# Masks of two query blocks made piece by piece between the steps of a graph attention layer

## The chip, the cores and the metric

The kernel runs on 1 core of a Trainium2 chip. The metric is device time in microseconds (us) of one execution, the median of several runs. Engines are TensorE (PE, matrix products and transposes), VectorE (DVE), ScalarE (ACT), GpSimd (POOL) and SyncE (SP, which here issues most DMA transfers).

## The reference

Eight graphs of 2048 nodes with 256 channels share one adjacency matrix of 2048 x 2048. For each graph, masked self-attention of 8 heads, then a residual, a layer norm, a feed-forward block of two layers, a second residual and norm, and an outer residual and norm:

```python
qkv = jnp.einsum('fnc,ck->fnk', x, w_qkv)            # f 8, n 2048, c 256
scores = jnp.einsum('fnhd,fmhd->fhnm', q, k) / jnp.sqrt(D)
scores = jnp.where((adj > 0)[None, None], scores, -1e9)
attn = softmax(scores, axis=-1)
t = jnp.einsum('fhnm,fmhd->fnhd', attn, v).reshape(F, N, C)
x1 = layernorm(x + t)
x2 = layernorm(x1 + relu(x1 @ w1 + b1) @ w2 + b2)
out = layernorm(x + x2)
```

The mask is the same for all graphs and heads. The kernel needs it turned: key nodes on the partitions, query nodes along the row.

## The kernel before

**Steps.** The work is cut into 1024 items `(f, qc, g, mb)`: 8 graphs `f`, 4 query blocks `qc` of 512 nodes, 2 groups `g` of 4 heads, 16 key blocks `mb` of 128 nodes. One pass of the main loop is one step `t`; a graph is 128 steps (`FRAME`), a group 16. In step `t` the kernel first lets waiting side work go on (`advance`), then issues the exponentials of item `t+1` (ACT, L237), the score products of item `t+2` (PE, L230; VectorE adds the mask to the scores as it moves them out of PSUM, L233, in two halves), the products with the values of item `t` (PE, L249), and the summing of the exponentials for the denominators (`add_up`): some blocks added by POOL (L271), some by an accumulating DMA that POOL issues (`p<-p`, L268), for `mb` 4, 5, 7, 9, 11 and 13.

**Side work.** Turning the input, projecting queries, keys and values, denominators, division, norms and the feed-forward block are Python generators kept in the list `fill`, sorted by due step. `start(t, gen, due)` adds one. A generator yields a number (go on so many steps later), `BANK` (it wants the spare PSUM bank, of which the main loop leaves one, so at most one such unit starts per step), `MORE` (it holds that bank and has more matmuls) and a few other conditions. `advance` hands out work as long as a credit of TensorE time lasts (`STEP` is added per step). With `finish=True` the credit is not asked. Nothing of this runs on the chip: it sets the order in which each engine's instructions stand, and every engine takes its own in that order. SP's transfers stand in one such order too, and a transfer that must wait holds up those behind it.

**When side work begins.** The table `NEXT` names the steps of a graph in which units for the next graph are started: turns of the input (`turn`), query projections (`ask`), key and value projections of node block `c` and group `g` (`project`). `kp` and `vp` hold 11 key and 11 value tiles in rotation, 8 for a graph and 3 of the next one.

**Masks.** `begin` (L559) makes the masks before the loop. For each of the 16 squares `(qc, c)` of 512 x 512 an SP transfer loads the adjacency into a `p` tile (L565), VectorE turns it into a code in bf16 (L582, two instructions), and `mask_blocks` (L132) transposes it on PE in two banks of eight 128 x 128 blocks (L141), moved out as 8-bit codes by ACT (L147) and VectorE (L145), and stored to the DRAM buffer `MD` (L148). While `qc` is 0 and 1, the turns and projections of the first graph stand between the squares; after `(1, 3)` the scores of the first two items and the first exponential are issued, and then follow the eight squares of `qc` 2 and 3 by themselves. The first query block's masks stay in SBUF; the others are fetched from `MD` by `load_mask` (L150), for query block `qc+1` in every second step of `qc`'s second group (`mb` odd, L607).

**Outcome.** When a block of queries is done, `outcome` (L333) takes a `y` tile (two in the pool), and `tail` (L359) runs its norms and `feed_forward` through the spare bank: two transposes of `y`, two units of the first layer, two of the second.

Of the kernel before, what the change touches and what calls it, by code (L numbers as in the profile page):

```python
# [10 lines left out]
F32 = mybir.dt.float32  # L11
BF16 = mybir.dt.bfloat16
I32 = mybir.dt.int32
I8 = mybir.dt.int8
F8 = mybir.dt.float8e5
AF = mybir.ActivationFunctionType
ALU = mybir.AluOpType
AX = mybir.AxisListType

P = 128  # L20
H = 8
D = 32
CH = 512
# [6 lines left out]
BANK, MORE, WAIT, TURNED, ROOM, INPUTS = -1, -2, -3, -4, -5, -10  # L30
STEP, UNIT, TURN, KEPT = 2200, 1024, 1400, 2200

MASKED = -57344.0
CODE = -5.0
# [27 lines left out]
def fast_path(ctx, tc, cst, x, adj, out, RS):  # L62
    nc = tc.nc
    F, N, C = x.shape
    NCK, TPC, MB = N // CH, CH // P, N // P
# [5 lines left out]
    kp = ctx.enter_context(tc.tile_pool(name="kp", bufs=3 * NCK - 1))  # L71
    qp = ctx.enter_context(tc.tile_pool(name="qp", bufs=4))
    vp = ctx.enter_context(tc.tile_pool(name="vp", bufs=3 * NCK - 1))
    pp = ctx.enter_context(tc.tile_pool(name="pp", bufs=12))
    work = ctx.enter_context(tc.tile_pool(name="work", bufs=1))
    yp = ctx.enter_context(tc.tile_pool(name="yp", bufs=2))
# [25 lines left out]
    def bank(dt=F32):  # L102
        shape = [P, CH] if dt == F32 else [P, 2, CH]
        if state["side"] is not None:
            i = 1 - state["side"]
            return ps_x[i].tile(shape, dt, name=f"x{i}")
        i = state["turn"]
        state["turn"] = (i + 1) % 5
        pool = ps_s[i] if i < 3 else ps_x[i - 3]
        return pool.tile(shape, dt, name=f"s{i}" if i < 3 else f"x{i - 3}")  # L110
# [11 lines left out]


    MD = dp.tile([NCK, MB // 2, P, 2 * CH // 4], I32, name="md")
    MK = {}

    def words(mask):
        return mask.rearrange("p b q -> p (b q)").bitcast(I32)
# [5 lines left out]
    def mask_blocks(qc, mc, cv, to=None):  # L134
        for half in range(2):
            yield BANK
            ps = bank(BF16)
            for r in range(2):
                for j in range(TPC):
                    rr = 2 * half + r  # L140
                    nc.tensor.transpose(ps[:, r, j * P:(j + 1) * P], cv[:, j, rr * P:(rr + 1) * P], identb)  # L141
            k = 2 * mc + half
            m = to[half] if to else mask_piece(0, qc, k)
            if half:
                nc.vector.tensor_tensor(m, ps, cst["ones"][:, 0:1, None].to_broadcast([P, 2, CH]), ALU.min, saturate=False)  # L145
            else:
                nc.scalar.copy(m.bitcast(I8), ps)  # L147
            nc.sync.dma_start(MD[qc, k], words(m))  # L148

    def load_mask(f, qc, k):  # L150
        nc.sync.dma_start(words(mask_piece(f, qc, k)), MD[qc, k])
# [343 lines left out]
    def start(t, gen, due):  # L495
        fill.append([t, gen, 1, due])
        fill.sort(key=lambda e: e[3])
# [13 lines left out]
    def advance(t, finish=False):  # L511
        state["credit"] = min(max(state["credit"], 0) + STEP, KEPT)
        state["now"] = t
        free = not state["holder"]

        def more():
            if state["holder"] and state["holder"][2] == WAIT:
                return False
            due = [e[3] for e in fill if e[2] == BANK and e[0] <= t or e is state["holder"]]
            return finish or state["credit"] >= UNIT or min(due) <= t  # L520

        if state["holder"]:
            resume(state["holder"], t)
            while state["holder"] and more():
                resume(state["holder"], t)
        inputs = True
        for e in list(fill):
            while e[2] is not None and e[0] <= t and e is not state["holder"]:
                if e[2] == BANK:
                    if not free or not more():  # L530
                        break
                    free = False
                elif e[2] < INPUTS:
                    inputs = inputs and not any(u is not None for u in live[:INPUTS - e[2]])
                    if not inputs:
                        break
                elif e[2] == TURNED and state["turned"] or e[2] == ROOM and state["tails"] == 2:
                    break
                resume(e, t)
            while e is state["holder"] and more():  # L540
                resume(e, t)
# [6 lines left out]
    def ask(f, c):  # L548
# [5 lines left out]
            60: [(project, 1, 0)], 66: [(ask, 3)], 72: [(turn, 3)], 80: [(project, 2, 0)], 98: [(ask, 0)], 100: [(project, 3, 0)],  # L554
            104: [(project, 0, 1)], 108: [(project, 1, 1)], 112: [(project, 2, 1)], 116: [(project, 3, 1)]}

    def begin():
        todo = deque((qc, c) for qc in range(NCK) for c in range(NCK))
        rows, cols = [], deque()  # L559

        def fetch():
            if todo:
                qc, c = todo.popleft()
                t = pp.tile([P, 4, CH], F32, name="p").bitcast(I32)
                nc.sync.dma_start(t, adj[qc * CH:(qc + 1) * CH, c * CH:(c + 1) * CH].rearrange("(j p) m -> p j m", p=P))  # L565
                cols.append((qc, c, t))

        for c in range(NCK):
            rows.append(pp.tile([P, 4, CH], F32, name="p"))
            xc = rows[c][:, 0:2, :].rearrange("p a (b c) -> p (a b) c", c=C)  # L570
            nc.sync.dma_start(xc, x[0, c * CH:(c + 1) * CH, :].rearrange("(j p) c -> p j c", p=P))
            fetch()
        fetch()
        while cols:
            qc, c, col = cols.popleft()
            if c % 2 == 0:
                two = pp.tile([P, 4, CH], F32, name="p").rearrange("p a q -> p (a q)").bitcast(BF16)
            cv = two[:, c % 2 * TPC * CH:(c % 2 + 1) * TPC * CH].rearrange("p (j m) -> p j m", m=CH)

            for half, what in enumerate((CODE, MASKED)):  # L580
                part = slice(half * 2 * P, (half + 1) * 2 * P)
                nc.vector.tensor_scalar(cv[:, :, part], col[:, :, part], 0.0, what, op0=ALU.is_le, op1=ALU.mult)  # L582
            fetch()
            xT = rows[c][:, 2:4, :]
            if qc == 0:
                yield from turn_rows(rows[c][:, 0:2, :].rearrange("p a (b c) -> p (a b) c", c=C), xT)
                nc.sync.dma_start(XD[0][c], xT)
                XT[0, c] = xT
                if c == 0:
                    yield from queries(0, 0, xT)  # L590
                yield from project(0, c, 0, xT)
            elif qc == 1:
                yield from project(0, c, 1, xT)
            if qc and c % 2 == 0:
                out4 = take([P, 4, 2, CH], F8)
                give(out4)
            yield from mask_blocks(qc, c, cv, [out4[:, c % 2 * 2 + i] for i in range(2)] if qc else None)
            if (qc, c) == (1, NCK - 1):
                for k in range(LEAD):
                    scores(items[k])  # L600
                exponentials(items[0])

    for _ in begin():
        pass
    state["side"] = 0
    for t, (f, qc, g, mb) in enumerate(items):
        if g == 1 and mb % 2 and (f + 1 < F or qc + 1 < NCK):  # L607
            load_mask(f + (qc + 1) // NCK, (qc + 1) % NCK, mb // 2)
        for what, *which in NEXT.get(t % FRAME, []):
            to = f if what is ask and which[0] else f + 1  # L610
            if to < F:
                at = (0, 0, 0) if what is turn else (which[0], 0, 0) if what is ask else (0, which[1], which[0] * TPC)
                start(t, what(to, *which), t + 3 * MB if what is turn else items.index((to, *at)) - LEAD - 1)
        if t == len(items) - MB // 2:
            xr, xb = state["rows"] = [take([P, TPC, C], F32) for _ in range(2)]
            nc.sync.dma_start(xr, x[f, qc * CH:(qc + 1) * CH, :].rearrange("(p j) c -> p j c", p=P))
        if t == len(items) - 2:
            nc.gpsimd.tensor_tensor(xb, xr, rows(cst["be2r"]), ALU.add)
        if t:
            advance(t)  # L620

        if t + 1 < len(items):
            exponentials(items[t + 1])
        if t + LEAD < len(items):
            nf, _, ng, nmb = items[t + LEAD]
            t0 = t
            while (nf, nmb // TPC, ng) not in V:
                advance(t0, finish=True)
                t0 += 1
            scores(items[t + LEAD])  # L630
        values(items[t])
        add_up(items[t])
        if mb == LAST and t + 1 < len(items):
            start(t + 2, denominator(f, qc, g, t + SUM), t + SUM + 4)
        if t == len(items) - 3:
            start(t, denominator(f, qc, g, t), t)
# [245 lines left out]
```

## Time and profile before

| | us |
|---|---|
| median of 3 runs | 3190.41 (3189.46 to 3194.38) |
| the profiled execution | 3196.28 |
| its span, first to last instruction | 3194.5 |
| TensorE busy (mean granted clock 0.987) | 3081.7 |
| VectorE busy | 2749.6 |
| ScalarE busy | 2417.7 |
| GpSimd busy | 2593.3 |

The profile page shows one execution: the busy share of each engine, the span in 40 slices with a digit for tenths, the DMA queues, the groups of instructions by line with count, busy time, mean length in ns, and the idle time before them with what ended it. The timeline lists instructions by start and length. The chain that ended last covers only the last microseconds here, with 0% at every name, so the stages are read from windows and from the timeline. Times of one step are differences between the starts of successive exponentials (L237).

### The profile page before, as it was taken

Reading aid. Unit: us, or ns where it says so; the run is one execution under the profiler, and the core shown is the slowest. Engines: PE = TensorE matmul, PEld = TensorE weight load, DVE = VectorE, ACT = ScalarE, POOL = GpSimd, SP = SyncE. Lnnn points to the kernel's source line nnn. Section 1 sums busy time; section 2 is a strip of 40 time slices with the busy share of each in tenths; the row PEclk is TensorE's granted clock in tenths of the full one; section 3 lists DMA queues with packets and bytes.
Section 4 is the critical chain, followed back from the end, with each engine's and each line's share of the span. In section 5 each row is a group of like instructions: output and inputs, shape, how many; then the busy total and the mean of one; then the engine's idle time right before and its main releaser. Section 6 shows DMA issues by size and latency. Waiting matters only on the chain. (4 is left out here: it accounts for less than half of the span.)

```text
span 3194.5 us, 68226 instructions
## 1 busy us (share of the span) xinstructions
PE 3081.7 (96%) x28868; PEld 963.0 (30%) x28868; DVE 2749.6 (86%) x3139; ACT 2417.7 (76%) x1909; POOL 2593.3 (81%) x1361
## 2 busy tenths in 40 slices
PE   7899999999999999999999999999999999999985
PEld 4222333222332223332333323323233233332222
DVE  4798988888889988889988988988988888889985
ACT  3677778777787777788777788778778778777774
POOL 0578888788888888888888888888889788889875
PEclk8899999999999999999999999999999999999998
DMA  9688889788798888898888899888879788888872
GB/s 323 142 192 193 183 175 199 161 188 189 179 195 188 191 194 178 176 204 196 187 177 174 194 208 198 168 182 196 196 174 203 177 196 192 176 177 166 178 150 64
DMA packets 153096, 589.46 MB, mean 185 GB/s; under 512 B 15024, under 2 KB 67760, under 8 KB 103888
## 3 DMA queue, kind: packets, MB, share of 16 engines
q0 software_dynamic: 64128, 433.22, 68.8%
q1 hardware_dynamic: 87840, 150.50, 13.7%
q8 instruction: 228, 3.74, 0.4%
q10 hardware_dynamic: 816, 1.31, 0.1%
q14 instruction: 84, 0.69, 0.1%
HBM read 146.67 MB, written 37.75 MB: 58 GB/s over the span
## 5 line engine op out<-in xcount | busy, mean ns | idle before, releaser
L233 DVE TENSOR_TENSOR p<-s,mask 128x1024 f32<-128x1024 f32 x2048 | 2409.1, 1218 | 325.0 <-PE s L230 182.9
L237 ACT ACTIVATE p<-p 128x2048 f32<-128x2048 f32 x1024 | 1956.0, 1910 | 566.5 <-DVE p L233 481.1
L271 POOL TENSOR_TENSOR p<-p 128x2048 f32<-128x2048 f32 x382 | 1875.4, 4909 | 359.1 <-ACT p L237 358.8
L230 PE MATMUL s<-qT,kT 32*128 32x512 f32 x8192 | 1172.5, 642 | 44.2 <-DVE p L233 39.4
L249 PE MATMUL x<-p,v 128*32 128x512 f32 x8192 | 1093.5, 606 | 4.6 <-ACT p L237 4.6
L230 PEld LDWEIGHTS s<-qT,kT 32*128 32x128 f32 x8192 | 320.9, 183 | 671.3 <-DVE p L233 643.6
L268 POOL DMA_DIRECT2D p<-p x382 | 416.8, 1092 | 70.1 <-ACT p L237 46.4
L249 PEld LDWEIGHTS x<-p,v 128*32 128x32 f32 x8192 | 161.5, 108 | 784.0 <-issue 310.2
L315 PE MATMUL x<-p,halves 128*32 128x512 f32 x2080 | 269.9, 595 | 0.0
L54 PE MATMUL x<-in,wqkv 128*32 128x512 f32 x1888 | 245.7, 592 | 0.0
L290 ACT ACTIVATE y<-y,nb,rs 128x256 f32<-128x256 f32 x372 | 219.1, 591 | 6.1 <-POOL nb L287 5.9
L278 DVE BATCH_NORM_STATS2 st<-y 128x6 f32<-128x256 f32 x372 | 155.0, 417 | 1.8 <-POOL y L370 1.8
L54 PE MATMUL x<-turned,w1s 128*32 128x512 f32 x992 | 123.9, 593 | 0.0
L54 PE MATMUL x<-w2s,hT 128*32 128x256 f32 x2016 | 121.8, 382 | 0.0
L54 PEld LDWEIGHTS x<-wqkv,in 128*32 128x32 f32 x3584 | 102.2, 110 | 64.1 <-issue 55.9
L54 PE MATMUL x<-wqkv,in 128*32 128x128 f32 x3584 | 117.4, 273 | 0.0
L315 PEld LDWEIGHTS x<-p,halves 128*32 128x32 f32 x2080 | 67.9, 111 | 156.9 <-issue 155.5
L368 POOL TENSOR_TENSOR y<-y,g2r 128x1024 f32<-128x1024 f32 x31 | 101.6, 3278 | 6.4 <-ACT y L290 6.4
L54 PEld LDWEIGHTS x<-in,wqkv 128*32 128x32 f32 x1888 | 61.3, 110 | 141.3 <-issue 116.5
L284 POOL TENSOR_TENSOR rs<-rs,mhalf 128x4 f32<-128x4 f32 x93 | 96.3, 1035 | 7.8
L370 POOL TENSOR_TENSOR y<-y,be2r 128x1024 f32<-128x1024 f32 x30 | 94.6, 3155 | 0.4
L54 PEld LDWEIGHTS x<-w2s,hT 128*32 128x32 f32 x2016 | 65.9, 111 | 70.7 <-issue 38.5
(121 smaller groups left out, 1301.1 us busy)
## 6 DMA issues: line engine op xcount, KB each, us to landing
p<-p POOLq DMA_DIRECT2D x382, 1024.0 KB, 10.0
in<-xd SPq DMA_DIRECT2D x87, 512.0 KB, 8.9
mask<-md SPq DMA_DIRECT2D x248, 128.0 KB, 8.6
y<-in_x_dram POOLq DMA_DIRECT2D x61, 512.0 KB, 10.1
p<-in_adj_dram SPq DMA_DIRECT2D x16, 1024.0 KB, 9.3
out_dram<-y SPq DMA_DIRECT2D x31, 512.0 KB, 6.2
in<-in_x_dram SPq DMA_DIRECT2D x30, 512.0 KB, 10.6
xd<-in SPq DMA_DIRECT2D x28, 512.0 KB, 8.8
```

Source lines behind the costliest of these rows:

```text
L54: nc.tensor.matmul(out[r:r + D], lhsT[:, r:r + D], rhs, start=start, stop=stop)
L230: nc.tensor.matmul(ps2[half][:, j, :], KT[f, mb // TPC, g][r:r + D, (mb % TPC) * P:(mb % TPC + 1) * P], QT[f, qc, g][r:r + D, :], start=Tr ...
L233: nc.vector.tensor_tensor(pt[:, 2 * half:2 * half + 2, :], ps, MK[f, qc, mb // 2][:, mb % 2, None, :].to_broadcast([P, 2, CH]), ALU.add)
L237: nc.scalar.activation(PT[item], PT[item], AF.Exp, scale=1.0 / math.sqrt(D))
L249: nc.tensor.matmul(O[grp][r:r + D, :], V[f, mb // TPC, g][:, mb % TPC, r:r + D], PT[item][:, h, :], start=(mb == 0), stop=(mb == LAST))
L268: nc.gpsimd.dma_start(PT[f, qc, g, chain[0]], PT.pop(item), accum_op=ALU.add)
L271: nc.gpsimd.tensor_tensor(first, first, PT.pop(item), ALU.add)
L278: nc.vector.bn_stats(st, t[:, j, :])
L284: nc.gpsimd.tensor_tensor(rs, rs, cst["mhalf"], ALU.pow)
L290: nc.scalar.activation(t[:, j, :], t[:, j, :], AF.Identity, bias=nb[:, j:j + 1], scale=rs[:, j:j + 1])
L315: nc.tensor.matmul(ps[r:r + D, :], cst["halves"][:, g, :], term[:, h, :], start=(n == 0), stop=(n == len(blocks) - 1))
L368: nc.gpsimd.tensor_tensor(z, z, rows(cst["g2r"]), ALU.mult)
```

## The change

The squares of query blocks 2 and 3 leave `begin`. They are made instead in 32 pieces of 512 queries x 128 keys by a new generator, `mask_job`, started every 2.25 steps from step 2 of the first graph. A piece works in one of four spare buffers, taken from a `spare` list: one key tile, one value tile, and the two halves of one `y` tile. It loads 128 keys of 512 rows of the adjacency (SP), three steps later casts the integers to bf16 in place (ACT), transposes four blocks through the spare bank (PE), makes the code (VectorE, into a part of the same buffer) and stores it to `MD` (SP); three steps later the buffer goes back. For the second sixteen pieces only the key and the value tile go back, so that the `y` tile is free for the second block's outcome. `MADE` lists the masks that stand in `MD`; before `load_mask` the loop runs `advance` with `finish=True` until the two it needs are in it. In the first graph the table `LATER` takes the place of some entries of `NEXT`: key and value projections begin up to 20 steps later.

```diff
-    MK = {}
+    MK, MADE, spare = {}, {(qc, b) for qc in range(2) for b in range(MB)}, deque()
...
+    def mask_job(n):
+        while not spare:
+            yield 1
+        part = spare.popleft()
+        qc, b = divmod(n + 2 * MB, MB)
+        col = part.bitcast(I32).rearrange("p (j m) -> p j m", j=TPC)
+        nc.sync.dma_start(col, adj[qc * CH:(qc + 1) * CH, b * P:(b + 1) * P].rearrange("(j p) m -> p j m", p=P))
+        yield 3
+        cv = part.bitcast(BF16)[:, 0:CH]
+        nc.scalar.copy(cv, part.bitcast(I32))
+        yield 1
+        yield BANK
+        ps = bank(BF16)[:, 0, :]
+        state["credit"] -= TURN // 2
+        for j in range(TPC):
+            nc.tensor.transpose(ps[:, j * P:(j + 1) * P], cv[:, j * P:(j + 1) * P], identb)
+        m = part[:, CH // 2:3 * CH // 4].bitcast(F8)
+        nc.vector.tensor_scalar(m.bitcast(I8), ps, 0.0, CODE, op0=ALU.is_le, op1=ALU.mult)
+        yield 1
+        nc.sync.dma_start(MD[qc, b // 2, :, b % 2 * P:(b % 2 + 1) * P], m.bitcast(I32))
+        MADE.add((qc, b))
+        yield 3
+        if n < MB or any(part is u for u in parts[0:2]):
+            spare.append(part)
...
+    LATER = {80: [], 100: [(project, 2, 0)], 104: [(project, 3, 0)], 108: [(project, 0, 1)], 112: [(project, 1, 1)],
+             116: [(project, 2, 1)], 120: [(project, 3, 1)]}
+
     def begin():
-        todo = deque((qc, c) for qc in range(NCK) for c in range(NCK))
+        todo = deque((qc, c) for qc in range(2) for c in range(NCK))
...
+    n_mask = 0
+    both = yp.tile([P, TPC, C], F32, name="y").rearrange("p j c -> p (j c)")
+    parts = [kp.tile([P, CH], F32, name="kT"), vp.tile([P, TPC, P], F32, name="v").rearrange("p j c -> p (j c)"),
+             both[:, 0:CH], both[:, CH:2 * CH]]
+    spare.extend(parts)
     for t, (f, qc, g, mb) in enumerate(items):
         if g == 1 and mb % 2 and (f + 1 < F or qc + 1 < NCK):
+            t0 = t
+            while not {((qc + 1) % NCK, b) for b in (mb - 1, mb)} <= MADE:
+                advance(t0, finish=True)
+                t0 += 1
             load_mask(f + (qc + 1) // NCK, (qc + 1) % NCK, mb // 2)
-        for what, *which in NEXT.get(t % FRAME, []):
+        while n_mask < 2 * MB and t >= 2 + 9 * n_mask // 4:
+            start(t, mask_job(n_mask), 3 * MB - 2 + n_mask if n_mask < MB else 4 * MB - 2 + n_mask)
+            n_mask += 1
+        for what, *which in (NEXT if f else {**NEXT, **LATER}).get(t % FRAME, []):
```

## The prediction

> **What bounds the kernel now.** I read the page's slices first, then a table of windows, the timeline of the opening, the groups by line, and last the DMA section. The slices:
>
> ```profile
> PE   7899999999999999999999999999999999999985
> ...
> DVE  4798988888889988889988988988988888889985
> ...
> PEclk8899999999999999999999999999999999999998
> ```
>
> From the third slice on TensorE is full and VectorE nearly so; only the ends are loose. The windows (busy us and instruction count of each engine, granted clock, DMA share, GB/s) show how loose the opening is:
>
> ```profile
> 60.00:80.00 20.00, 9.64 (x72) 7.01 (x72) 13.27 (x16) 5.88 (x5) 0.00 (x0) 0.53 0.82 289
> 80.00:100.00 20.00, 11.01 (x80) 7.22 (x80) 12.15 (x15) 5.93 (x6) 0.00 (x0) 0.50 0.29 88
> ...
> 240.00:280.00 40.00, 38.82 (x344) 11.50 (x340) 33.94 (x31) 33.47 (x27) 35.80 (x14) 1.00 0.93 214
> ```
>
> For 40 us TensorE is half busy at half clock and POOL idle: this is where the masks of query blocks three and four are made. One round in the timeline (start, length, engine, line):
>
> ```profile
> 77.25 1.28 DVE L582 TENSOR_SCALAR p<-p 128x1024 bf16<-128x1024 int32 x2
> ...
> 77.99 1.89 PE L141 MATMUL x<-identb,p 128*128 128x128 bf16 x16 [1.98 <-DVE p L582]
> 79.06 1.01 ACT L147 CAST in<-x 128x1024 int8<-128x1024 bf16 x1 [2.81 <-PE x L141]
> 79.92 1.23 DVE L145 TENSOR_TENSOR in<-x,ones 128x1024 fp8e5<-128x1024 bf16 x1 [1.38 <-PE x L141]
> 81.06 1.29 DVE L582 TENSOR_SCALAR p<-p 128x1024 bf16<-128x1024 int32 x2
> ```
>
> A round is 3.8 us, and there are eight. In the groups by line these price a step and the work that resembles a piece:
>
> ```profile
> L233 DVE TENSOR_TENSOR p<-s,mask 128x1024 f32<-128x1024 f32 x2048 | 2409.1, 1218 | 325.0 <-PE s L230 182.9 <-issue 33.2 <-ACT y L290 30.1
> ...
> L356 DVE TENSOR_TENSOR y<-x,rc 128x512 f32<-128x512 f32 x63 | 42.7, 678 | 0.0
> ```
>
> Two L233 adds are 2.44 us, the floor of one of the 1024 steps; steps with other TensorE work go above it. Differences between starts of successive L237 exponentials give the step: 2.56 us where nothing is slipped in (19 steps of the first graph), 2.93 with half a projection, 3.79 with the second feed-forward block, and 2.86 where four transposes are followed by L356 (61 steps).
>
> **The change, part by part.** The sum is made against the profiled execution, 3196.28 us (span 3194.5), which is 5.9 above the median of 3190.41.
>
> (1) The opening loses its eight rounds. VectorE ends the second item's adds at 65.9, and the third item's scores start at 96.55: -30.6 us. Steps right after it run at half clock in both, since the clock falls at 61.35 before the rounds begin; if it also returns some 2 us later than the 6 it took before (96.5 to 102.3), the gain is 29. I keep -30.6.
>
> (2) In the steps come 32 pieces: an ACT cast of 128x512, four bf16 transposes, a VectorE pass of 128x512 from PSUM. VectorE's is half of L145's 1.22, so 0.61; TensorE's, from eight such transposes in 0.61, about 0.36; ACT's near 0.57, in ACT's idle time (ACT is busy 76%). Nearest row: the L356 step, 2.86 against 2.56, so 0.30 each, 9.6 for 32. Bounds: 0 (all in VectorE's idle 14%) and 0.61 x 32 = 19.5 (VectorE the floor in each).
>
> (3) In the built order, 26 pieces stand one to a step. From the seventeenth on, only the key and value tiles return to the spare list, so a new piece starts about every four steps where the plan wants one per 2.25. The fourth block's masks are thus not made when `load_mask` asks, and the loop runs everything pending on the spot: two pieces in step 89, two in 91, two in 93, the last in 95. Step 91 also takes two y transposes, two x transposes, the whole first feed-forward layer and half of the second; step 93 a key and value projection, the other half and a norm. All go one after another through the single spare bank, TensorE waiting for each eviction. By rows:
> - Step 89: adds in front 1.5, two pieces (0.36 + 0.61 and the handover) 1.7, half projection 0.97, scores 0.99, values 0.92: 6.1.
> - Step 91: three transposes with evictions (0.66; 0.77, 0.77, 0.58) and the L290 activates ahead of them on ACT 4.9; two first-layer blocks with eviction 5.4; second layer 1.95 and its L490 add 0.7; two pieces 2.0; transposes 0.6; scores and values 1.9: 17.5.
> - Step 93: keys 2.55, second layer 2.6, statistics 4 x 0.6, POOL's chain 1.65, an activate 0.6, cast 0.55, pieces and scores and values 3.35: 13.7.
> - Step 95: the last piece's load can start only when its tile's store has landed; some 5 for the store behind a p<-p transfer and 4 to 5 for the load keep the cast, and TensorE behind it, some 6 past its time: 9.0.
>
> The same work spread over steps costs only its excess over an empty one. Step 91's is 3.95 by the means above, step 93's 2.66; with the slots of 89 and 95 and the pieces already in (2), the loss is 2.6 + 10.4 + 7.9 + 6.1 = 27. Bounds: 15 (evictions overlap) and 45 (each round also waits for store, mask load and next load in turn, 8 to 9 each by the DMA rows).
>
> (4) Clock. Inside steps 91 to 95 TensorE is a third to half busy. At 57.6 to 61.35 us one such stretch, 1.14 busy, was enough for the granted clock to go to 0.50, and half-busy work kept it there until 102.3. The chains of (3) hold some 14 us of matmuls that would take 14 more at half clock; I take half, 7; bounds 0 and 20 (the scores and values of these steps too).
>
> [...]
>
> (5) Late loads. A piece is cast on ACT three steps, 8.7 us, after its load is planned, and the exponentials queue behind that cast. It moves 512 rows of 512 B. The DMA section:
>
> ```profile
> p<-p POOLq DMA_DIRECT2D x382, 1024.0 KB, 10.0
> ...
> mask<-md SPq DMA_DIRECT2D x248, 128.0 KB, 8.6
> ...
> in<-in_x_dram SPq DMA_DIRECT2D x30, 512.0 KB, 10.6
> ```
>
> The x load also has 512 rows. Its 29 landings in the steps, from the trace's issue and landing records, run from 3.5 to 21.4 us, eleven of them above 14, when p<-p transfers and other loads are in flight. Even five steps of lead were twice not enough in the second graph:
>
> ```profile
> 610.76 1.03 PE L95 MATMUL x<-ident,in 128*128 128x128 f32 x4 [4.06 <-DMA in<-in_x_dram]
> ...
> 649.95 1.09 PE L95 MATMUL x<-ident,in 128*128 128x128 f32 x4 [3.49 <-DMA in<-in_x_dram]
> ```
>
> With ACT's slack of 1.4 a wait begins at 10.1; averaged over the 29 that is 3.0 us per group of loads, and the order on SP has about seven groups with three or four steps of lead, some of them 11 us, so 14 rather than 21. What waits behind a late cast: the next exponential, the values matmul that needs it, and all of TensorE. SP's queue suffers too: a store waits for VectorE, the next load for that store's landing, and mask loads and reloads stand behind both; these have 8 to 16 steps, and I cost that at nothing (up to 10 if the cover goes). Bounds of (5): 0 and 45.
>
> [...]
>
> (6) The second graph. Before, it takes 391.7 us from first to last exponential start; the third to seventh take 379.4 to 381.2. Its excess is the two waits shown and the half clock after each. The pieces push its work a few steps, and in the built order it then stands as in the fourth graph on all engines from step 151 on, with x loads and turns where they never waited: -11 (bounds -12 and 0). Reordering in the third adds 1.
>
> Sum: -30.6 + 9.6 + 27 + 7 + 14 - 11 + 1 = +17 us. On the profiled 3196.3 that is 3213; on the median, 3207.
>
> **The rivals.**
> A. Every piece is on time: loads land as in the quiet rows (3.5 to 8.7 us). Then (5), the clock loss (4) and step 95's wait go, 27 us together, and the sum is -10: 3180. It decides once these three together cost under 3.6, since 0.2% is 6.4 us. For it: pieces are cut small and SP runs ahead. Against: p<-p holds the engines 68.8% of the span.
> B. The queue itself becomes the bound. The windows already have a DMA share of 0.8 to 0.9; 26 loads with 32 packets per engine come at three to five per group of 16 steps, and if they clear only between p<-p transfers, each of the six groups waits some 7 us instead of 2.3: +28, so 3235. For it: one x load at 628.8 landed only at 649.8. Against: a stalled TensorE also stops p<-p, and packets of 1024 B then pass in 0.05 us.
> C. VectorE is the floor in every piece's step: +10, 3217, inside the forecast's range. That the second graph's waits stay adds 11 likewise. That the work isn't moved is excluded by the built order.
>
> **How the numbers follow.** Forecast 0.50, with its own range 3196 to 3225 ((2), (4) and (5) each a third of the way to its bounds); A 0.30; B 0.20. About 0.2% is what a measurement here can tell from no change. Of A, 0.24 lies below 3184 and 0.06 within; of the forecast 0.04 within. So faster 0.24, same 0.10, slower 0.66. The range goes down to 3168 (A with (2) and (3) near their lower bounds) and up to 3252 (B with (3) half way up); I leave some 0.06 beyond each end.
>
> **What would show it.** (1) The third item's scores at about 66 us. (2) Steps with a lone piece near 2.86. (3) Steps 89 to 95 taking near 54 us instead of 20, plus (4), with half clock in them. (5) ACT casts of pieces waiting for DMA before steps 27, 35, 46 and 53. (6) No wait of L95 for x in the second graph. The forecast is wrong if steps 91 and 93 pass in under 10 us each, or if casts never wait.

## The result

| | before | after |
|---|---|---|
| median, us (six runs each) | 3190.4 (3187.7 to 3197.4) | 3217.4 (3213.8 to 3221.4) |
| profiled execution, us | 3196.28 | 3213.83 |
| its span, us | 3194.5 | 3211.6 |

The kernel became slower: ratio 1.0081, 95% interval 1.0068 to 1.0094. Between the two profiled executions the difference is +17.6 us, and that is the one that can be traced. Between the medians it is +27.0, because the profile before lies 5.9 above its median and the profile after, the fastest of its six runs, 3.6 below its own. In three later sets of runs, on three chips, the kernel before had medians of 3193.98, 3194.72 and 3194.11 us (27, 14 and 15 runs); against those, 3217.4 is roughly +23. Why the other runs after lie above the profiled one was not traced.

The slices of the page after, first:

```profile
PE   7899799999999999999999999999999999999985
...
DVE  4889588889888889899888889888988888889985
...
PEclk9999899999999999999999999999999999999998
```

The second slice is fuller on VectorE than before, and the clock, at half for 41 us of the opening before, is at half for 3.4 us there. In place of that the fifth slice (321 to 401 us, steps 85 to 98) has 7 tenths of TensorE, 5 of VectorE and a granted clock of 0.85. The windows after (busy us and count of PE, PEld, DVE, ACT, POOL; granted clock; DMA share; GB/s) show both ends of that trade:

```profile
60.00:80.00 20.00, 15.99 (x112) 3.92 (x116) 17.98 (x16) 13.66 (x8) 6.35 (x3) 0.91 0.39 106
80.00:100.00 20.00, 17.93 (x151) 4.46 (x144) 18.03 (x18) 14.81 (x13) 16.68 (x7) 1.00 1.04 211
...
345.00:367.00 22.00, 16.18 (x104) 5.24 (x108) 4.31 (x5) 7.77 (x12) 7.50 (x5) 0.69 0.71 187
367.00:380.00 13.00, 7.93 (x132) 3.56 (x128) 5.34 (x13) 4.90 (x7) 5.83 (x6) 0.99 0.12 32
380.00:392.00 12.00, 6.10 (x36) 1.49 (x36) 5.93 (x6) 5.27 (x6) 8.74 (x3) 0.82 0.56 127
```

Where the time went, by the starts of the exponentials (L237 before, L262 after; "items a to b" runs from the start of item a's exponential to the start of item b's, and step `i` below is the time from item `i` to the next; all in us):

| stretch | before | after | change | predicted |
|---|---|---|---|---|
| start to item 2 | 101.1 | 68.2 | -32.9 | -30.6 |
| items 2 to 88 | 242.2 | 261.5 | +19.3 | +21.5: 25 pieces x 0.30, loads 14 |
| items 88 to 97 | 26.4 | 67.8 | +41.4 | +36.1: 27, 7 pieces x 0.30, clock 7 |
| items 97 to 128 | 92.5 | 90.3 | -2.2 | 0 |
| second graph | 391.7 | 381.6 | -10.1 | -11 |
| third graph | 379.4 | 381.6 | +2.2 | +1 |
| the rest | 1961.2 | 1960.6 | -0.6 | 0 |

The longest single loss is step 91, from the exponential at 341.97 to the next at 363.74. The timeline of TensorE and VectorE in it, without the weight loads (start, length, engine, line; idle time before it and its releaser):

```profile
343.31 0.66 PE L95 MATMUL x<-ident,y 128*128 128x128 f32 x4
...
345.09 0.66 PE L95 MATMUL x<-ident,y 128*128 128x128 f32 x4 [1.12 <-ACT turned L489]
...
346.61 1.11 PE L95 MATMUL x<-ident,in 128*128 128x128 f32 x4 [0.87 <-ACT turned L489]
...
348.40 3.64 PE L54 MATMUL x<-turned,w1s 128*32 128x512 f32 x16 [0.68 <-ACT in L191]
...
352.85 3.64 PE L54 MATMUL x<-turned,w1s 128*32 128x512 f32 x16 [0.81 <-ACT hT L502]
...
357.29 1.93 PE L54 MATMUL x<-w2s,hT 128*32 128x256 f32 x32 [0.81 <-ACT hT L502]
...
359.36 0.69 DVE L515 TENSOR_TENSOR y<-x,y 128x512 f32<-128x512 f32 x1 [14.55 <-PE x L54]
360.11 0.38 PE L165 MATMUL x<-identb,v 128*128 128x128 bf16 x4 [0.88 <-DVE y L515]
360.59 0.69 DVE L167 TENSOR_SCALAR v<-x 128x512 int8<-128x512 bf16 x1 [0.53 <-PE x L165]
361.33 0.38 PE L165 MATMUL x<-identb,kT 128*128 128x128 bf16 x4 [0.84 <-DVE v L167]
```

This is the forced work in one spare bank: every unit on PE waits 0.7 to 1.1 us for the eviction of the unit before it, and VectorE has nothing to do for 14.55 us, because no scores are behind it yet. The clock fell at 346.66 for 10.2 us. The two first-layer blocks therefore take 3.64 us each; the same chain at full clock is shown with the run noloads below, and there they take 1.92 us.

The other loss is in the casts that wait for their loads. The ACT timeline after:

```profile
97.05 0.62 ACT L159 CAST y<-y 128x512 bf16<-128x512 int32 x1 [3.08 <-DMA y<-in_adj_dram]
...
149.88 0.62 ACT L159 CAST v<-v 128x512 bf16<-128x512 int32 x1 [6.97 <-DMA v<-in_adj_dram]
155.89 0.62 ACT L159 CAST y<-y 128x512 bf16<-128x512 int32 x1 [3.58 <-DMA y<-in_adj_dram]
...
214.16 0.62 ACT L159 CAST v<-v 128x512 bf16<-128x512 int32 x1 [5.10 <-DMA v<-in_adj_dram]
```

With four smaller ones (1.37 at 116.4, 1.42 at 164.3, 0.97 at 358.7, 4.34 at 391.7) these waits are 26.8 us in sum. By the trace's issue and landing records the 32 loads took 2.2 to 18.4 us to land, ten of them more than 8.7, which is the time of three steps. The wait at 391.7 is another kind: its load landed 2.5 us after issue, but was issued late. SP's queue shows the store of the same tile, then a mask load that waited 6.9 us for that store to land, and the load behind both:

```profile
380.55 0.34 SPq L169 DMA_DIRECT2D md<-v  x1
387.87 0.34 SPq L176 DMA_DIRECT2D mask<-md  x1
388.30 0.38 SPq L169 DMA_DIRECT2D md<-kT  x1
388.79 0.38 SPq L156 DMA_DIRECT2D v<-in_adj_dram  x1
```

### The profile page after: what moved, and what is told of

It reads as the page before. It is cut to its first block, busy times and chain, and to the rows that moved or that the text cites. A ratio compares the mean times of both kernels' runs of the same rounds, so it can differ in the third digit from the quotient of the medians.

```text
span 3211.6 us, 68385 instructions
## 1 busy us (share of the span) xinstructions
PE 3086.2 (96%) x28868; PEld 956.8 (30%) x28868; DVE 2748.3 (86%) x3147; ACT 2425.9 (76%) x1933; POOL 2593.4 (81%) x1361
## 5 line engine op out<-in xcount | busy, mean ns | idle before, releaser
L262 ACT ACTIVATE p<-p 128x2048 f32<-128x2048 f32 x1024 | 1955.7, 1910 | 556.0 <-DVE p L258 459.1
L293 POOL DMA_DIRECT2D p<-p x382 | 410.3, 1076 | 76.7 <-ACT p L262 48.2
L54 PE MATMUL x<-turned,w1s 128*32 128x512 f32 (+1 forms) x1024 | 129.1, 600 | 2.1 <-ACT hT L502 0.8
## 6 DMA issues: line engine op xcount, KB each, us to landing
p<-p POOLq DMA_DIRECT2D x382, 1024.0 KB, 10.1
```

The lines of the kernel that those rows point to most:

```text
L54: nc.tensor.matmul(out[r:r + D], lhsT[:, r:r + D], rhs, start=start, stop=stop)
L262: nc.scalar.activation(PT[item], PT[item], AF.Exp, scale=1.0 / math.sqrt(D))
L293: nc.gpsimd.dma_start(PT[f, qc, g, chain[0]], PT.pop(item), accum_op=ALU.add)
```

## The experiments

Ratios are to the kernel before on the same chip, with their 95% intervals. A segment is a difference of exponential starts in the profiled run, as in the table above.

**later: the table alone.** The masks stay in the opening as before; only the later starts of key and value projections in the first graph are taken over.

```diff
-        for what, *which in NEXT.get(t % FRAME, []):
+        for what, *which in (NEXT if f else {**NEXT, **LATER}).get(t % FRAME, []):
```

> The kernel before with the table LATER alone (no pieces; all masks in the opening). In the built order the second graph then stands as the later ones do. If the two waits for x in the second graph belong to its order and are there in unprofiled runs too: 3179 to 3185 us, and the second graph takes 381 us from first to last exponential start instead of 391.7. If they were an accident of the profiled execution: 3190, as before.

Measured: 3186.33 us, ratio 0.9972 [0.9961, 0.9982], on a before of 3193.98; that is 1.3 above the interval I gave, which was worked out from the lower before of 3190.4. The second graph takes 381.6 us, as in the changed kernel, and the opening, items 2 to 88 and 88 to 97 stay within 1.6 us of before. So the order alone is enough for the -10 of the second graph, without any piece. It is not a fixed gain: no run with the table has a wait for x in the second graph, but that graph takes between 381.6 and 388.0 us in them. Where before waited 4.06 and 3.49 us for x at 610 and 650, the windows of this run show a TensorE that is full:

```profile
590.00:630.00 40.00, 39.40 (x316) 10.73 (x312) 36.25 (x39) 33.33 (x28) 35.73 (x23) 1.00 0.86 189
630.00:670.00 40.00, 40.00 (x412) 12.93 (x408) 34.70 (x41) 31.48 (x26) 33.14 (x16) 1.00 0.84 196
```

**noloads: the pieces without their loads.** Only the first four pieces load; the masks of query blocks three and four are zeros.

```diff
-        nc.sync.dma_start(col, adj[...])
+        if n < 4:
+            nc.sync.dma_start(col, adj[...])
...
-        nc.vector.tensor_scalar(m.bitcast(I8), ps, 0.0, CODE, op0=ALU.is_le, op1=ALU.mult)
+        nc.vector.tensor_scalar(m.bitcast(I8), ps, 0.0, 0.0, op0=ALU.is_le, op1=ALU.mult)
```

> The changed kernel with only the first load of each of the four buffers; the other 28 pieces cast what is left there and write a mask of zeros, so the third and fourth block's masks are left out. All casts, transposes, evictions and stores stay. Theory (late loads hold ACT and TensorE): the waits of the casts go, some 14 us in the lone pieces and some 10 in the forced steps: about 3193. Rival (the forced steps cost by their serial chain alone): 3203, steps 89 to 96 still above 45 us. Rival (the work of the pieces on VectorE and TensorE): 3215.

Measured: 3193.98, ratio 0.9998 [0.9988, 1.0008]. The time is what I gave for late loads alone, but the stretches are not. Between the spans of the profiled runs that is 19.6 us less than the changed kernel. Items 2 to 88 fall from 261.5 to 249.9 us: 11.6 go with the loads, and 7.8 stay over before, for the 25 pieces and what moved with them (one of the four loads that are left is late too: a cast at 97.9 waits 3.10). Items 88 to 97 fall only from 67.8 to 60.1: of the 41.4 there, 33.7 stand without any load. The 7.7 that go are 3.9 in step 91, 4.3 in step 95 and 1.3 in step 96, less 1.6 in step 90, which is longer here. Of these steps only 95 holds a long wait for a load, the 4.34 above. Step 93 takes 13.8 us against 14.0, and step 91, between these exponentials, 17.9 against 21.8:

```profile
331.56 1.91 ACT L263 ACTIVATE p<-p 128x2048 f32<-128x2048 f32 x1
349.44 1.91 ACT L263 ACTIVATE p<-p 128x2048 f32<-128x2048 f32 x1
```

TensorE's timeline there is the chain of the changed kernel with the same waits, one unit after another, but at full clock:

```profile
332.89 0.66 PE L95 MATMUL x<-ident,y 128*128 128x128 f32 x4
334.68 0.65 PE L95 MATMUL x<-ident,y 128*128 128x128 f32 x4 [1.13 <-ACT turned L490]
336.20 0.65 PE L95 MATMUL x<-ident,in 128*128 128x128 f32 x4 [0.87 <-ACT turned L490]
337.53 1.92 PE L54 MATMUL x<-turned,w1s 128*32 128x512 f32 x16 [0.68 <-ACT in L192]
340.26 1.92 PE L54 MATMUL x<-turned,w1s 128*32 128x512 f32 x16 [0.81 <-ACT hT L503]
```

The two first-layer blocks are 1.72 us shorter each and the third transpose 0.46, together 3.9. So step 91 is 17.9 us of serial chain and 3.9 of clock. For the stretch as a whole this run speaks for the chain and against late loads as its main cause.

**pieces24: no forced steps.** The last eight pieces are left out, and the second half of the fourth query block uses the third block's masks.

```diff
-        while n_mask < 2 * MB and t >= 2 + 9 * n_mask // 4:
+        while n_mask < MB + MB // 2 and t >= 2 + 9 * n_mask // 4:
```

> The changed kernel without the last eight pieces (the fourth block's second eight key blocks use the third block's masks), so that no step is forced. Theory (forced steps lose some 40 us): 3175 to 3182, faster than before. Rival (cost goes with the number of pieces): 3206 to 3211.

Measured: 3181.5, ratio 0.9961 [0.9944, 0.9978]; some 36 us under the changed kernel between the medians, of which the eight pieces themselves are 2.4 at 0.30 each. Items 88 to 97 take 26.0 us, less than the 26.4 of before, while the casts still wait 18.8 us in sum and items 2 to 88 take 260.7; the second graph takes 388.0. The exponentials of items 88 and 97:

```profile
331.05 1.90 ACT L262 ACTIVATE p<-p 128x2048 f32<-128x2048 f32 x1
...
357.10 1.91 ACT L262 ACTIVATE p<-p 128x2048 f32<-128x2048 f32 x1 [0.63 <-DVE p L258]
```

The forced steps, not the pieces as such, made the change a loss.

**half16: half the pieces.** Query block three goes back into the opening; sixteen pieces remain, one per 3.25 steps.

```diff
-        todo = deque((qc, c) for qc in range(2) for c in range(NCK))
+        todo = deque((qc, c) for qc in range(3) for c in range(NCK))
...
-        while n_mask < 2 * MB and t >= 2 + 9 * n_mask // 4:
+        while n_mask < MB and t >= 2 + 13 * n_mask // 4:
```

> Half the change: the third block's masks back in the opening, the fourth's in 16 pieces over all four buffers, one started every 3.25 steps; no step is forced. Theory: opening -15 to -17, pieces +5, late loads 0 to +8, second graph -5 to -11: 3170 to 3183. Rival (cost goes with the number of pieces): 3204.

Measured: 3186.21, ratio 0.9972 [0.9962, 0.9983]: not better than the table LATER alone, and above my interval. There are no forced steps, and the opening gains 15.7 us. But two casts wait 2.7 and 7.4 us, items 2 to 88 take 254.8 us instead of 242.2, and the second graph takes 385.1. With half as many loads the three slowest still took 11.4, 13.0 and 18.1 us to land; that led to the runs that follow.

**half16_lead6, half16_lead3: when the cast comes.** half16_lead6 has three edits at once: six steps from load to cast, earlier starts, and buffers that all come back until step 42. half16_lead3 puts only the first one back.

```diff
# half16_lead6, against half16
-        yield 3
+        yield 6
...
-        if n < MB or any(part is u for u in parts[0:2]):
+        if state["now"] < 42 or any(part is u for u in parts[0:2]):
...
-        while n_mask < MB and t >= 2 + 13 * n_mask // 4:
+        while n_mask < MB and t >= 2 + 5 * n_mask // 2:
# half16_lead3, against half16_lead6
-        yield 6
+        yield 3
```

> Sixteen pieces as in half16, but each is cast six steps after its load is planned instead of three, with one started every 2.5 steps. Theory (a load is late by its landing time, some 10 to 20 us beside the p<-p transfers, and a longer lead hides it): the casts' waits of 10.1 us in half16 go to under 2, and the time to 3174 to 3179. Rival (the DMA queue cannot carry the loads at all, so they are as late whatever the lead): the waits stay above 8, 3186.

> As half16_lead6, with one number put back: the cast comes three steps after the load again, and not six; rate of starts and return of buffers stay. Theory (the six steps of lead removed the casts' waits for late loads): the waits come back, about 10 us in sum as in half16 instead of 2.7, so some 7 to 12 us over half16_lead6: 3180 to 3186 on a before of 3194, ratio 0.9955 to 0.9975. Rival (the earlier starts and the return of the y buffers made the gain, the lead nothing): 3172 to 3176, ratio 0.993.

Measured: 3173.75, ratio 0.9932 [0.9918, 0.9945], with the lead; 3190.14, ratio 0.9990 [0.9981, 0.9999], without it, above the 3180 to 3186 I had expected. The single number is worth 16 us between the medians; between the profiled runs 14.8 in items 2 to 72, and 10.0 in all. The ACT timeline of half16_lead3 has this,

```profile
168.72 0.62 ACT L159 CAST v<-v 128x512 bf16<-128x512 int32 x1 [8.45 <-DMA v<-in_adj_dram]
176.82 0.62 ACT L159 CAST y<-y 128x512 bf16<-128x512 int32 x1 [5.67 <-DMA y<-in_adj_dram]
```

and that of half16_lead6 one wait in all:

```profile
177.28 0.62 ACT L159 CAST v<-v 128x512 bf16<-128x512 int32 x1 [2.73 <-DMA v<-in_adj_dram]
```

The loads themselves are no faster: the three slowest land 15.8, 19.1 and 11.8 us after issue with three steps of lead, and 18.7, 15.0 and 10.4 with six. The windows of half16_lead3 show what a late cast takes with it: from 165 to 180 us, with 9.4 of the 14.1 us of these two waits inside, TensorE is busy for 7.00 of 15.00, at clock 0.61.

```profile
165.00:180.00 15.00, 7.00 (x32) 1.93 (x32) 3.74 (x4) 5.61 (x5) 4.51 (x1) 0.61 0.81 192
```

**p24_lead7, p24_lead3, p28_lead5: more pieces.** Two of the eight squares stay in the opening, the other 24 pieces are made in the steps, with four more buffers (the halves of the work tiles "turned" and "hT"), and seven steps of lead. p24_lead3 differs from it in that number alone. p28_lead5 leaves one square, with 28 pieces and five steps.

```diff
# p24_lead7, against the changed kernel
-        yield 3
+        yield 7
...
-        if n < MB or any(part is u for u in parts[0:2]):
+        if state["now"] < 46 or any(part is u for u in parts[0:2]):
...
-        todo = deque((qc, c) for qc in range(2) for c in range(NCK))
+        todo = deque((qc, c) for qc in range(3) for c in range(NCK) if qc < 2 or c < 2)
...
-    n_mask = 0
+    n_mask = 8
...
+    for name in ("turned", "hT"):
+        w = work.tile([P, 2, CH], F32, name=name)
+        parts += [w[:, 0, :], w[:, 1, :]]
...
-        while n_mask < 2 * MB and t >= 2 + 9 * n_mask // 4:
+        while n_mask < 2 * MB and t >= 2 + 2 * (n_mask - 8):
```

> Twenty-four pieces (two squares of the third block stay in the opening), eight buffers until step 46 (also the halves of the two work tiles, idle until the first feed-forward block), cast seven steps after the load is planned; no step is forced. Theory: opening -23, order of the second graph -9, pieces +7, waits of casts under 3: 3165 to 3172. Rival (the queue carries no more): waits above 10, 3178 to 3185.

> As p24_lead7, with one number put back: three steps from load to cast instead of seven. Theory: with 24 pieces and loads close together the casts wait 10 to 20 us in sum instead of 0.9, so 3181 to 3193 on a before of 3194, ratio 0.9958 to 0.9995. Rival (the eight buffers, not the lead, made it good): 3170 to 3176, ratio 0.993.

> Twenty-eight pieces (one square of the third block stays in the opening), eight buffers until step 46, cast five steps after the load is planned; no step is forced. Theory: opening -27, order -3 to -9, pieces +8.4, waits of casts 0 to 6: 3165 to 3178. Rival (the queue carries no more): waits above 12, 3182 or more.

Measured: p24_lead7 3172.51, ratio 0.9930 [0.9917, 0.9944], half a microsecond above what I expected and the lowest median of all, though not told apart from half16_lead6; p24_lead3 3184.06, ratio 0.9965 [0.9952, 0.9979]; p28_lead5 3176.62, ratio 0.9939 [0.9925, 0.9952]. The casts wait 0.9, 12.8 and 6.3 us in that order. Seven steps instead of three are worth 11.6 us. In p24_lead7 the stretch where the changed kernel ran its forced steps is full:

```profile
330.00:360.00 30.00, 30.00 (x280) 9.46 (x280) 24.41 (x24) 23.77 (x21) 24.85 (x12) 1.00 0.72 163
360.00:400.00 40.00, 39.62 (x364) 12.29 (x356) 37.25 (x45) 30.47 (x24) 35.01 (x19) 1.00 0.91 205
```

Its second graph still takes 386.7 us. Step by step against its own fourth graph, 4.6 us of that lie in steps 138, 141, 151 and 156, half of it in step 151 (4.96 against 2.61); what held these steps was not followed.

**p32_eight: all 32 pieces, eight buffers, five steps of lead.**

```diff
# against p24_lead7
-        yield 7
+        yield 5
...
-        todo = deque((qc, c) for qc in range(3) for c in range(NCK) if qc < 2 or c < 2)
+        todo = deque((qc, c) for qc in range(2) for c in range(NCK))
...
-        while n_mask < 2 * MB and t >= 2 + 2 * (n_mask - 8):
-            start(t, mask_job(n_mask), 3 * MB - 2 + n_mask if n_mask < MB else 4 * MB - 2 + n_mask)
+        while n_mask < 2 * MB and t >= 2 + 3 * n_mask // 2:
+            start(t, mask_job(n_mask), 3 * MB - 2 + n_mask)
```

(`n_mask` starts at 0.)

> All 32 pieces, eight buffers until step 46, cast five steps after the load is planned, one started every 1.5 steps; only step 95 is forced, with two pieces and three quarters of the first feed-forward layer. Theory (the loss of the change is its forced steps and late loads): opening -31, order -9, pieces +9.6, the one forced step some +8, waits 0 to 6: 3170 to 3178. Rival (32 pieces in the steps cost more than the opening by their work): 3190 or more.

Measured: 3188.45, ratio 0.9984 [0.9975, 0.9994], well above what I expected. The casts wait 6.2 us, which I had allowed for. What I had not: a borrowed work tile is wanted again by the first feed-forward block while its mask is still being stored. The timeline of this run (the store into DRAM on SP's queue, and the activate on ACT):

```profile
221.67 0.32 SPq L169 DMA_DIRECT2D md<-turned  x1
224.53 0.32 SPq L169 DMA_DIRECT2D md<-turned  x1
...
239.08 0.78 ACT L489 ACTIVATE turned<-x,be1c,g1c 128x512 f32<-128x512 f32 x1 [7.51 <-DMA md<-turned]
```

The second store landed 14.1 us after its issue. The last piece is still forced into step 95 (8.9 us between the exponentials at 350.58 and 359.47). Items 97 to 128 take 98.2 us instead of 92.5: step 100 takes 4.72 against 2.95, with a whole feed-forward unit in it, and step 127 takes 6.66 against 3.29, where an activate ahead of the exponential waits 3.67 us for POOL. What pushed this work there was not tested.

## Why the prediction was right, point by point

The sum was +17 on the profiled execution, and the two profiles differ by 17.6. That closeness is luck. The parts are off by up to 5.3 us and cancel, and the profile after happens to be the fastest of six runs; on the medians I forecast 3207, and 3217.4 was measured, 10 us above and inside the range. What held is the mechanism: forced steps, late loads and the clock cost more than the opening gave.

1. *The opening, -30.6.* It gained 32.9: the third item's exponential starts at 68.2 instead of 101.1. I had let half clock last as long after these scores as before. In the changed kernel half clock from 63.35 lasts 3.4 us; the stretch of 41 us before, at half clock with TensorE busy for 23.0 of it, was gone.
2. *The pieces, 0.30 each.* Steps with a lone piece and nothing late take mostly 2.80 to 2.88 us against 2.56, so 0.24 to 0.32; here are steps 40 and 41:

```profile
183.88 1.91 ACT L262 ACTIVATE p<-p 128x2048 f32<-128x2048 f32 x1 [0.97 <-DVE p L258]
186.72 1.91 ACT L262 ACTIVATE p<-p 128x2048 f32<-128x2048 f32 x1 [0.93 <-PE s L255]
189.58 1.92 ACT L262 ACTIVATE p<-p 128x2048 f32<-128x2048 f32 x1 [0.95 <-PE s L255]
```

The eviction takes 0.69 (estimated 0.61) and the cast 0.62 (0.57). With VectorE as the floor such a step would take 2.44 + 0.69 = 3.13; it does not, so rival C falls, though its 3217 happens to be the measured median.
3. *The forced steps, 27, and 4. their clock, 7.* The steps took 6.1 us (the step from item 90, where what was forced in step 89 shows; predicted 6.1), 21.8 (91, 17.5), 14.0 (93, 13.7), and steps 94, 95 and the one behind them 16.3 (9.0 for step 95 and two ordinary ones of 2.56 make 14.1). At full clock the chain of step 91 was sized right: noloads takes 17.9 for it. Clock cost 3.9 in that step, where the two first-layer blocks were stretched by 1.7 each and a transpose by 0.5. It was at half three times more in the stretch, from 363.73, 380.79 and 391.03. What these cost is not shown by a run; half of TensorE's busy time at half clock in the stretch is about 10 us, an estimate from the trace and an upper bound. With my 46.3 for the four steps, 7 for the clock and five other steps of 2.56 to 2.93, the stretch comes to 66 to 68 us, and it took 67.8. What I mis-sized is the term that I took off, 7.0 for the same work when it is spread (0.4, 3.95 and 2.66 in steps 89, 91 and 93): before, the nine steps of this stretch took 26.4, only 3.4 over nine empty ones, so only 3.4 was there to be saved in it. Another 2.2 came back in items 97 to 128. Hence 41.4 against 36.1, or 39.2 with what came back.
5. *Late loads, 14.* noloads gives 11.6 in the ordinary steps. The longest waits came at steps 28, 29 and 48, near two of the four I had named (27 and 46), none at 35 and 53, and smaller ones at 11, 18 and 32. Of the x landings that I went by, ten are above 14 us and not eleven, which changes nothing in the sum. The mechanism, three steps of lead against landings of up to 18 us, is what the two pairs of runs with one number changed show: 16.4 and 11.6 us between medians.
6. *The second graph, -11; the third, +1.* -10.1 and +2.2. The cause as I put it, pieces that push the work, was not needed: the table LATER does it without any piece (later: 381.6 as well). The 391.7 runs to the first exponential of the next graph, not to the last of its own.

Rival A (pieces on time, 3180) needed loads that land in 8.7 us and casts that never wait; half16_lead6 and p24_lead7, where the lead covers the landings, show that the idea pays once that is so. Rival B (each group waiting some 7 us) was reached by one cast, 6.97; the next are 5.10 and 4.34.

At 346.66 the clock fell after 3.41 us in which TensorE was busy for 1.42, with no gap above 1.12 us in the rows shown; at 61.35 before, it was 1.14 of the 3.41. The chain of noloads, with the same gaps, kept its clock: from 335 to 347 us TensorE was busy for 7.15 of 12.00, at 1.00. By the rows of noloads the 3.41 us up to 336.96 hold only 1.30 of work, and full clock stayed, so the busy time just ahead does not tell the two apart; what decided between them was not tested by a run. Half clock lasted 3.4 us from 63.35, 216.95 and 363.73, with TensorE busy for 3.10, 3.42 and 3.41 of it, and 10.2 us from 346.66, with 8.34 busy; before, it lasted 41.0 us from 61.35, with 22.96.

The medians of the piece loads after, by group, are 6.5 to 7.9 us from issue to landing; ten of the 32 took more than 8.7 us and the slowest 18.4, and these set the waits.

The groups of piece loads after, with their median us from issue to landing:

```profile
kT<-in_adj_dram SPq DMA_DIRECT2D x11, 256.0 KB, 6.5
v<-in_adj_dram SPq DMA_DIRECT2D x11, 256.0 KB, 7.9
y<-in_adj_dram SPq DMA_DIRECT2D x10, 256.0 KB, 7.3
```

## What to carry to other kernels

When work is moved from an idle stretch into the gaps of a full pipeline, lay out the resulting order first and look for steps where a deadline runs everything pending at once: here the stretch of nine steps around four such ones took 41 us more, against the 33 that the opening gained. Give a load the lead of its slowest landing beside the other transfers, not of its median: one number, three steps to six or seven, was worth 12 to 16 us with nothing else changed. And try each part of a change by itself: the small reordering of projections alone was worth 0.28%, hidden here by the losses.

## What was not expected of the hardware

A stall on one engine brought a second loss with it. Every wait of a cast of 5 us or more for its load in items 2 to 72 (in the changed kernel, half16, half16_lead3, pieces24 and p24_lead3) came with half clock on TensorE, which set in during the wait or within 3 us of its end and lasted 3.4 to 10.2 us: at 148.7 and 217.0 after, 174.6 in half16, 163.8 and 177.5 in half16_lead3, 150.8 and 215.6 in pieces24, 168.3 in p24_lead3.

A store of only 64 KB took 14.1 us to land beside the other transfers (p32_eight), so that a borrowed buffer comes free as late as a load arrives.
